# A transformer block in float32 on one core: the two-input instructions of VectorE in another form, GpSimd's order written down, and norms made a tile earlier

## The chip, the core and the metric

The kernel runs on one core of a Trainium2 chip. The metric is the device time of one execution in microseconds (us), lower is better. A core has five engines that run side by side: TensorE (PE, matrix products; its weight loads are listed as PEld), VectorE (DVE), ScalarE (ACT), GpSimd (POOL) and SyncE (SP, which issues most DMAs). Each takes its instructions in one order that is fixed when the program is built, and semaphores make an engine wait for another. SBUF is the memory on chip that all engines work in, PSUM the one that TensorE writes to.

## What is computed

The input `x` has 4 sequences of 2048 tokens with 512 features, in float32. First comes causal attention with one head, then a feed-forward layer with two gates. Cut to what matters here:

```python
h = layernorm(x)
q, k, v = relu(h @ Wq + bq), relu(h @ Wk + bk), relu(h @ Wv + bv)
e = q @ k.T / sqrt(512) - 10000 * causal
y = softmax(e) @ v
x = x + layernorm(relu(y @ Wo + bo))
x = x + layernorm(ffn(layernorm(x)))   # two branches of 512 -> 128 features, softmax, top 32 of 512
```

## The kernel before

**Phases.** `phase1` does the attention, the first residual and the norms for the feed-forward layer; `phase2` does the feed-forward layer and the output. There is a second version of each behind a branch (`every_key=True`) for inputs whose scores could grow too large; it isn't run here.

**Groups.** Phase 1 works on 16 groups of 512 tokens (4 tiles of 128), four groups per sequence; a batch is one sequence here, and `n.g` counts a group in its batch from 0. Features lie on the partitions for q, k, v and scores. The head makes the first group's projections; then `steps` runs a loop over the groups. In one turn, for group `n`: the scores against its own keys (`score_tile`), those against earlier groups' keys, the products of the next group's v, q, k and vo, the maxima, the weights, and the product with the values.

**Products with seven parts.** Except in the head, each 512 x 512 x 512 product is made of seven products of 256-wide halves (`class Seven`, the Strassen-Winograd scheme), which need sums and differences of the halves of both operands. `token_sums`, `value_sums`, `key_sums`, `query_sums` and `last_query_sum` make those on VectorE, one difference each of tokens and queries (T4) on GpSimd. The pieces p1 to p7 are issued on TensorE in the order p2, p5, p1, p3, p6, p7, p4. Several accumulate into one PSUM tile (`acc`), which VectorE writes out in between (`written`, lines 590 and 594): p6, p7 and p4 of a product can't start before the write-out of the piece before.

**Softmax.** `masked` adds the causal mask to the diagonal block (line 680) and takes a running maximum (688); `maximum` does so for the other tiles (577). `fold` and `diagonals` bring the maximum to all partitions, `weights` subtracts it (725, VectorE), takes the exponential (726, ScalarE) and sums (728, 730, GpSimd). `inverses` and `attended` (758) scale the product with the values.

**The chain.** `chain` follows for each tile of a group, while the next group's products run: statistics and inverse root of the variance (`row_norm`: VectorE, then GpSimd at line 140), the norm (771, VectorE), the residual's add into `x1` (773, GpSimd), a second norm (145 to 149, 140, 781), products with the convolution's weights (789, GpSimd), their sums over four features (797, VectorE), transposes (793, 801) and stores. `fetch_features` loads the gates' features back, in another layout, and takes their statistics (276).

**Who sets the order.** TensorE's and VectorE's order in `steps` is the program's (`tc.manual_schedule`); the framework's scheduler orders the other engines. The program's order comes from a planner, `class Pace`. It keeps two clocks: `t`, which every product on TensorE advances, and `v`, VectorE's. VectorE's work is in generators that yield after each piece the piece's time and a pause until the next may come. `run` takes pieces that are due, from three ranks: rank 0 for write-outs and what TensorE waits for, rank 1 for maxima, weights and sums, rank 2 for the chains, of which the first two are open. `flush` issues what is left of a job. The planner knows nothing of what actually happens; it only decides the order.

**Other places.** `moments` takes the statistics of the inputs of the group after next; `transpose_x` makes the norm of the first two groups' tiles on VectorE (319) and transposes them on TensorE (167); later groups go through `turn_x` (328, 331) and DRAM. `prepare` runs in turns 1 and 2: it loads constants of phase 2, one of them (`left`, 859) by a DMA of GpSimd's queue, which VectorE then splits into three rows (862 to 867).

Of the kernel before, what the change touches and what calls it, by code (L numbers as in the profile page):

```python
# [39 lines left out]
P = 128  # L40
GT = 512
# [12 lines left out]
def sandwich_kernel(ctx: ExitStack, tc: tile.TileContext, io: dict, out: bass.AP):  # L54
# [144 lines left out]
    def phase1(every_key):  # L199
# [22 lines left out]
        class Pace:  # L222

            def __init__(self):
                self.t = self.v = 0.0
                self.ranks = [], [], []
# [9 lines left out]
            def step(self, job):  # L239
                try:  # L240
                    us, pause = next(job[1])
                    self.v = max(self.v, job[0]) + us
                    job[0] = self.v + pause
                except StopIteration:
                    for jobs in self.ranks:
                        jobs[:] = [j for j in jobs if j is not job]
# [25 lines left out]
        pace = Pace()  # L272

        def work(us, fn, *args, pause=0.0):

            fn(*args)
            yield us, pause

        def load(b, g):

            n = Group()
            n.b, n.g, n.i = b, g, b * GB + g
            n.x = []
            for t in range(TPG):
                xt = xp.tile([P, D], F32, name="xt")
                row = n.i * GT + t * P
                nc.sync.dma_start(xt, xf[row : row + P, :])
                n.x.append(xt)
            return n

        def moments(n, joint=True):

            n.rstd = sm.tile([P, TPG], F32, name="rstd_x")
            var = sm.tile([P, TPG], F32, name="var_x")
            n.mv = sm.tile([P, TPG, nc.vector.BN_AGGR_DIM], F32, name="mv_x")
            for t, xt in enumerate(n.x):
                st = sm.tile([P, nc.vector.BN_STATS_DIM], F32, name="st_x")
                nc.vector.bn_stats(st, xt)
                nc.vector.bn_aggr(n.mv[:, t, :], st)
                if not joint:  # L300
                    nc.vector.tensor_scalar_add(var[:, t : t + 1], n.mv[:, t, 1:2], LN_EPS)
                    inv_sqrt(n.rstd[:, t : t + 1], var[:, t : t + 1])
                yield 0.8, 0.0
            if joint:
                nc.vector.tensor_scalar_add(var, n.mv[:, :, 1], LN_EPS)  # L305
                inv_sqrt(n.rstd, var)
                yield 0.2, 1.0

        def at_once(pieces):
            for _ in pieces:  # L310
                pass

        def transpose_x(n, tiles=range(TPG)):

            for t in tiles:
                if t == 0:
                    n.xnT = one.tile([P, NC, GT], F32, name="xnT")
                xn = two.tile([P, D], F32, name="xn")
                nc.vector.tensor_scalar(
                    xn, n.x[t], n.mv[:, t, 0:1], n.rstd[:, t : t + 1], ALU.subtract, ALU.mult  # L320
                )
                transposed(ps_tp, xn, n.xnT[:, :, t * P : (t + 1) * P], nc.scalar.copy)

        def turn_x(n):

            for t in range(TPG):
                xn = two.tile([P, D], F32, name="xn")
                nc.vector.tensor_scalar(
                    xn, n.x[t], n.mv[:, t, 0:1], n.rstd[:, t : t + 1], ALU.subtract, ALU.mult
                )  # L330
# [112 lines left out]
        def token_sums(n):  # L443
# [5 lines left out]
            def pieces():  # L449
                nc.vector.tensor_tensor(T1, B12, B11, ALU.subtract)  # L450
                yield 0.75, 0.0
                nc.vector.tensor_tensor(T2, B22, T1, ALU.subtract)
                nc.gpsimd.tensor_tensor(T4, B21, T2, ALU.subtract)
                yield 0.75, 0.0
                nc.vector.tensor_tensor(B12, B22, B12, ALU.subtract)
                yield 0.75, 0.0
# [3 lines left out]
        def value_sums(n, most):  # L460
# [3 lines left out]
            if most:  # L464
                S1, S2 = (one.tile([P, 2, H], F32, name=f"T{k}") for k in (1, 2))
                n.left = {1: A11, 2: A12, 4: A22, 5: S1, 6: S2, 7: A21}
                nc.vector.tensor_tensor(S1, A21, A22, ALU.add)
                yield 0.9, 0.0
                nc.vector.tensor_tensor(S2, S1, A11, ALU.subtract)
                yield 0.9, 0.0  # L470
                nc.vector.tensor_tensor(A21, A11, A21, ALU.subtract)
                yield 0.9, 0.0
            else:
                n.left[3] = one.tile([P, 2, H], F32, name="T4")
                nc.vector.tensor_tensor(n.left[3], A12, n.left[6], ALU.subtract)
                yield 0.9, 0.0

        def key_sums(n):

            A11, A21, A12, A22 = quarters(n.kT)  # L480
            S1, S2, S4 = (one.tile([P, 2, H], F32, name=f"Q{k}") for k in (1, 2, 4))
            nc.vector.tensor_tensor(S1, A21, A22, ALU.add)
            yield 0.9, 0.0
            nc.vector.tensor_tensor(S2, S1, A11, ALU.subtract)
            yield 0.9, 0.0
            nc.vector.tensor_tensor(A21, A11, A21, ALU.subtract)
            yield 0.9, 0.0
            nc.vector.tensor_tensor(S4, A12, S2, ALU.subtract)
            for k, t in ((2, A12), (5, S1), (1, A11), (3, S4), (6, S2), (7, A21), (4, A22)):
# [3 lines left out]
        def query_sums(n):  # L493
# [3 lines left out]
            n.queries = {1: B11, 2: B21, 3: B22, 4: T4, 5: T1, 6: T2}  # L497
            nc.vector.tensor_tensor(T1, B12, B11, ALU.subtract)
            yield 0.9, 0.0
            nc.vector.tensor_tensor(T2, B22, T1, ALU.subtract)  # L500
            nc.gpsimd.tensor_tensor(T4, B21, T2, ALU.subtract)
            yield 0.9, 0.0

        def last_query_sum(n):

            B11, B12, B21, B22 = quarters(n.qT)
            nc.vector.tensor_tensor(B12, B22, B12, ALU.subtract)
            n.queries[7] = B12

        class Seven:  # L510
# [65 lines left out]
            def maximum(self, st):  # L576
                nc.vector.tensor_tensor(self.n.mx, self.n.mx, st, ALU.max)

# [96 lines left out]
        def masked(n, kt):  # L675
            st, off = n.st[kt], first(n, kt)
            own = kt - n.g * TPG
            if 0 <= own < TPG:
                q = slice(own * P, (own + 1) * P)
                nc.vector.tensor_tensor(st[:, q], st[:, q], causal, ALU.add)  # L680
            if every_key and own > 0:
# [5 lines left out]
            else:  # L687
                nc.vector.tensor_tensor(n.mx[:, off:], n.mx[:, off:], st[:, off:], ALU.max)

# [29 lines left out]
        def weights(n):  # L719

            n.sum = one.tile([P, GT], F32, name="mxsum")
            for kt in range(n.nk):
# [6 lines left out]
                else:  # L729
                    nc.gpsimd.tensor_tensor(n.sum[:, off:], n.sum[:, off:], w, ALU.add)  # L730
                yield 0.08 + (GT - off) / 960, 0.0

# [28 lines left out]
        def chain(n, t):  # L761
# [7 lines left out]
            m, r = row_norm(sm, a, "a")  # L769
            yield 1.0, 1.1  # L770
            nc.vector.tensor_scalar(a, a, m, r, ALU.subtract, ALU.mult)
# [4 lines left out]
            store.dma_start(x1_d[n.i][t * P : (t + 1) * P, :], x1)  # L776
            yield 0.55, 1.8
            m, r = row_norm(sm, x1, "x1")
            yield 1.0, 1.1
            xn2 = ap.tile([P, D], F32, name="a")  # L780
# [10 lines left out]
            if not final:  # L791

                nc.vector.transpose(a, xn2)
                nc.sync.dma_start(xn2T_d[n.i][t * P : (t + 1) * P, :], a)
            yield 1.4 if final else 0.7, 0.0 if final else 1.0
            for j, pr in enumerate(prs):
                nc.vector.tensor_reduce(xg[:, j, :], pr.rearrange("p (g f) -> p g f", f=CF), axis=AX.X, op=ALU.add)  # L797
                yield 0.68, 0.0 if final or j else 0.6
            if not final:
# [72 lines left out]
        def steps(n, ahead):  # L872
# [3 lines left out]
            for j in range(NGRP):  # L876
# [88 lines left out]

                pace.flush(weighted)
                if j in (1, 2):
                    next(early)
# [82 lines left out]
        else:  # L1051
# [4 lines left out]
            for m in "vqk":  # L1056
# [4 lines left out]
                drop(w)  # L1061
            w = project_vo(n)
            weight_sums("o", w)
            drop(w)
# [3 lines left out]
            for br in branches:  # L1068
# [303 lines left out]
```

## Time and profile before

| | |
|---|---|
| median of 3 runs | 2513.23 us (2512.48 to 2515.34) |
| profiled execution | 2513.1 us, of which span 2511.3 us from first to last instruction, TensorE's granted clock 0.988 |
| phase 1 / phase 2 | up to about 1813 us / the rest |

Busy time in some stretches of the span (us; a stretch is named by the groups' turns in it):

| stretch | long | PE | DVE | ACT | POOL |
|---|---|---|---|---|---|
| 0 to 90, head and first scores | 90 | 74.5 | 28.1 | 18.3 | 9.0 |
| 90 to 190 | 100 | 93.0 | 70.4 | 30.2 | 29.6 |
| 505 to 640 | 135 | 129.8 | 92.6 | 40.7 | 36.1 |
| 640 to 800 | 160 | 156.8 | 101.6 | 43.6 | 55.7 |
| 800 to 945 | 145 | 145.0 | 84.1 | 36.9 | 46.5 |
| 1760 to 2511, mostly phase 2 | 751 | 710.6 | 690.5 | 540.8 | 607.1 |

A row of the profile's tables of instructions names the line, the engine, the operation, the tile written and the tiles read (buffer numbers left out), the shapes and the count, and then busy time or durations. In the timeline, the first two numbers are start and duration in us, and the bracket at the end is the engine's idle time before the instruction with what ended it. In the waits, a row says who waited for whom, for how long in all, how often, and the longest. Durations come from one execution.

### The profile page before, as it was taken

What the parts mean: (1) busy time and instruction counts of PE and PEld (TensorE: products, weight loads), DVE (VectorE), ACT (ScalarE), POOL (GpSimd) and SP (SyncE); (2) the same over time, 40 slices, a digit from 0 to 9 for tenths busy, and PEclk for the clock granted to TensorE, in tenths of its full rate; (3) what the DMA queues carried; (4) which work ended last, traced back from release to release, by engine and by line L of the source; (5) the groups of instructions that cost most, each with busy time, mean ns of one, the idle gap of its engine ahead of it and who ended that gap; (6) DMA issues with size and microseconds to landing.
All of it is one profiled execution on the core that took longest, in us unless ns stands there. A gap on an engine that the chain in (4) does not pass through costs nothing.

```text
span 2511.3 us, 29224 instructions
## 1 busy us (share of the span) xinstructions
PE 2417.3 (96%) x8354; PEld 1520.5 (61%) x8354; DVE 1777.8 (71%) x3815; ACT 1026.5 (41%) x2232; POOL 1141.6 (45%) x1045
## 2 busy tenths in 40 slices
PE   8989999999999999899999999999899999999997
PEld 3666858587685858668585876856333333333332
DVE  2487675658766565866655577554599999999997
ACT  2323322232332223233131323312178787878785
POOL 1033240423324051342414134231278989898986
PEclk9999999999999999999999999999899999999998
DMA  6577656557765656776555576633424444444541
GB/s 208 165 218 212 196 154 173 147 180 216 208 192 158 169 147 181 225 207 197 162 162 157 175 222 192 190 119 74 122 71 102 110 106 119 107 119 105 120 107 56
DMA packets 594347, 392.18 MB, mean 156 GB/s; under 512 B 392705, under 2 KB 459777, under 8 KB 594177
## 3 DMA queue, kind: packets, MB, share of 16 engines
q1 hardware_dynamic: 590640, 387.05, 55.8%
q10 hardware_dynamic: 3024, 2.11, 0.3%
q8 instruction: 70, 1.15, 0.2%
q0 software_dynamic: 512, 1.06, 0.1%
q14 instruction: 101, 0.82, 0.1%
HBM read 275.26 MB, written 114.82 MB: 155 GB/s over the span
## 4 chain that ended last, share of the span: by engine, by line
PE 80%; DVE 6%; POOL 5%; ACT 4%; issue 4%; DMA 1%; SPq 1%; POOLq 0%; ACTq 0%; DVEq 0%
PE acc L542 20%; PE acc L743 19%; PE mm L542 14%; PE mm L1198 13%; PE mm L660 5%; PE lg L1156 3%; PE mm L397 2%; PE tp L1265 2%; PE lg L1159 1%; POOL e_si L1186 1%; POOL xs L1192 1%; POOL h L1305 1%; ACT L1136 1%; DVE xg L797 1%; POOL x L773 1%
## 5 line engine op out<-in xcount | busy, mean ns | idle before, releaser
L743 PE MATMUL acc<-vo,st 128*128 128x512 f32 x1088 | 474.7, 592 | 1.4 <-ACT st L726 1.4
L743 PEld LDWEIGHTS acc<-vo,st 128*128 128x128 f32 x1088 | 205.3, 190 | 241.5 <-issue 236.0
L1198 PE MATMUL mm<-w_L_ffn_weight,xnT 128*128 128x512 f32 x512 | 249.0, 609 | 0.5 <-ACT xc_si L817 0.5
L1198 PE MATMUL mm<-w_L_ffn_weight,xsT 128*128 128x512 f32 x512 | 239.1, 610 | 2.5 <-ACT xsT L1271 2.5
L140 POOL TENSOR_TENSOR rstd_x<-var_x,neg_half 128x4 f32<-128x4 f32 (+1 forms) x19 | 17.9, 943 | 424.6 <-DVE var_x L305 419.7
L542 PE MATMUL acc<-T,wb 128*128 128x256 f32 x720 | 174.0, 385 | 15.9 <-DVE vT L594 13.4
L140 POOL TENSOR_TENSOR rs_a<-ve_a,neg_half 128x1 f32<-128x1 f32 x64 | 39.2, 613 | 292.6 <-DVE ve_a L149 289.9
L542 PE MATMUL mm<-xnT,wb 128*128 128x256 f32 x720 | 171.1, 381 | 0.0
L730 POOL TENSOR_TENSOR mxsum<-mxsum,st 128x512 f32<-128x512 f32 (+2 forms) x144 | 161.5, 1121 | 13.8 <-ACT st L726 2.9
L542 PE MATMUL acc<-xnT,wb 128*128 128x256 f32 x720 | 165.2, 379 | 0.0
L542 PEld LDWEIGHTS acc<-T,wb 128*128 128x128 f32 x720 | 138.1, 193 | 43.9 <-DVE vT L594 15.0
L1198 PEld LDWEIGHTS mm<-w_L_ffn_weight,xsT 128*128 128x128 f32 x512 | 92.9, 191 | 110.3 <-issue 93.5
L1198 PEld LDWEIGHTS mm<-w_L_ffn_weight,xnT 128*128 128x128 f32 x512 | 92.3, 190 | 106.7 <-issue 106.0
L542 PEld LDWEIGHTS acc<-xnT,wb 128*128 128x128 f32 x720 | 136.8, 190 | 25.0 <-issue 4.3
L542 PEld LDWEIGHTS mm<-xnT,wb 128*128 128x128 f32 x720 | 136.5, 191 | 24.4 <-issue 7.2
L660 PE MATMUL mm<-qT,kT 128*128 128x128 f32 (+3 forms) x512 | 150.2, 437 | 0.0
L561 ACT COPY cp<-mm 128x512 f32<-128x512 f32 x72 | 42.2, 586 | 236.6 <-PE mm L542 236.6
L1164 DVE MAX8 m_si<-rest_si 128x8 f32<-128x512 f32 x192 | 131.3, 684 | 0.0
L1172 DVE MATCH_REPLACE8 rest_si<-m_si,rest_si 128x512 f32<-128x512 f32 x192 | 129.8, 676 | 0.0
L1164 DVE MAX8 m_so<-rest_so 128x8 f32<-128x512 f32 x192 | 129.8, 676 | 0.0
L1172 DVE MATCH_REPLACE8 rest_so<-m_so,rest_so 128x512 f32<-128x512 f32 x192 | 129.8, 676 | 0.0
L590 DVE TENSOR_TENSOR st<-acc,cp 128x256 f32<-128x256 f32 x144 | 54.1, 417 | 102.0 <-PE acc L542 97.9
(245 smaller groups left out, 5056.2 us busy)
## 6 DMA issues: line engine op xcount, KB each, us to landing
wb<-keys SPq DMA_DIRECT2D x168, 256.0 KB, 2.9
x<-x SPq DMA_DIRECT2D x124, 256.0 KB, 3.0
xt<-in_L_attn_x_dram SPq DMA_DIRECT2D x64, 256.0 KB, 3.6
xr<-in_L_attn_x_dram SPq DMA_DIRECT2D x64, 256.0 KB, 3.2
xn<-xn SPq DMA_DIRECT2D x64, 256.0 KB, 2.9
out_dram<-h SPq DMA_DIRECT2D x64, 256.0 KB, 2.0
wb<-Z_v SPq DMA_DIRECT2D x60, 256.0 KB, 3.2
wb<-Z_q SPq DMA_DIRECT2D x60, 256.0 KB, 3.0
```

The costliest lines, as they stand in the source:

```text
L140: nc.gpsimd.tensor_tensor(dst, src, neg_half[:, : src.shape[1]], ALU.pow)
L397: nc.tensor.matmul(ps, lhsT=w[c][1][:, d * P : (d + 1) * P], rhs=xnT[:, c, :], start=(c == 0), stop=(c == NC - 1))
L542: nc.tensor.matmul(ps[:, d * H : (d + 1) * H], lhsT=left[:, c, d * P : (d + 1) * P], rhs=right[:, c, :], start=(new and c + d == 0), stop= ...
L590: nc.vector.tensor_tensor(st[:, cols], acc[:, d, :], other[:, d, :], ALU.add)
L660: nc.tensor.matmul(ps[:, off:], lhsT=kT[:, c, k : k + P], rhs=n.qT[:, c, off:], start=(c == 0), stop=(c == NC - 1),)
L730: nc.gpsimd.tensor_tensor(n.sum[:, off:], n.sum[:, off:], w, ALU.add)
L743: nc.tensor.matmul(acc, lhsT=n.st[kt][:, t * P : (t + 1) * P], rhs=vos[kt // TPG][:, kt % TPG, :], start=(kt == 0), stop=(kt == nk - 1),)
L1156: nc.tensor.matmul(n.lg[br], lhsT=xa[n.k][br][:, n.t * P : (n.t + 1) * P], rhs=lin_T[br], start=True, stop=False)
L1164: nc.vector.max(n.m8[br], n.rest[br] if k else n.lg[br])
L1172: nc.vector.match_replace(n.rest[br], n.m8[br], n.rest[br], -LOWEST)
L1198: nc.tensor.matmul(ps, lhsT=lhsT[:, c, :], rhs=wf[:, c, :], start=(c == 0), stop=(c == NC - 1))
L1265: nc.tensor.transpose(tp[:, c, :], p.xs[:, c * P : (c + 1) * P], ident)
```

## The change

- A helper `combine(out, a, b, op)` issues `scalar_tensor_tensor` on VectorE, (a times 1.0) op b. In the groups' steps it takes the place of `tensor_tensor` wherever both inputs lie in SBUF: `token_sums`, `value_sums`, `key_sums`, `query_sums`, `last_query_sum`, `maximum` and `masked`. Instructions with an input in PSUM (590, 594, 725) stay, as do the head's `weight_sums` and phase 2.
- GpSimd joins the engines whose order in `steps` is the program's. The planner gets a third clock, `p`, GpSimd's; a piece may yield a tuple in place of its pause: the times of what it issues on GpSimd, of which the first is what the next piece waits for.
- The norms of the second group's tiles: two are made in the head, before `weight_sums("o", ...)`, and kept in `n.ahead`; in the loop each of the others is issued a tile before its transposes. The transposes of token tile `t` follow the scores of key tile `t`; before, those of tiles 0 and 1 followed key tile 0, those of 2 and 3 key tiles 1 and 2.
- The flush of the chains that are left of the group before (`behind`) and `fetch_features` move from before K's products to behind the flush of the weights.

```diff
             def step(self, job):
                 try:
-                    us, pause = next(job[1])
+                    us, behind = next(job[1])
                     self.v = max(self.v, job[0]) + us
-                    job[0] = self.v + pause
+                    job[0] = self.v + behind if isinstance(behind, float) else max(self.p, self.v + 0.2) + behind[0] + 0.1
+                    if not isinstance(behind, float):
+                        self.p = max(self.p, self.v + 0.2) + sum(behind)
...
+        def combine(out, a, b, op):
+
+            nc.vector.scalar_tensor_tensor(out, a, 1.0, b, ALU.mult, op)
...
             if joint:
                 nc.vector.tensor_scalar_add(var, n.mv[:, :, 1], LN_EPS)
                 inv_sqrt(n.rstd, var)
-                yield 0.2, 1.0
+                yield 0.2, (0.55,)
...
+        def normed(n, t):
+            xn = two.tile([P, D], F32, name="xn")
+            nc.vector.tensor_scalar(xn, n.x[t], n.mv[:, t, 0:1], n.rstd[:, t : t + 1], ALU.subtract, ALU.mult)
+            return xn
...
-                xn = two.tile([P, D], F32, name="xn")
-                nc.vector.tensor_scalar(
-                    xn, n.x[t], n.mv[:, t, 0:1], n.rstd[:, t : t + 1], ALU.subtract, ALU.mult
-                )
+                xn = n.ahead.pop(0) if n.ahead else normed(n, t)
                 transposed(ps_tp, xn, n.xnT[:, :, t * P : (t + 1) * P], nc.scalar.copy)
...
-                nc.vector.tensor_tensor(T2, B22, T1, ALU.subtract)
+                combine(T2, B22, T1, ALU.subtract)
                 nc.gpsimd.tensor_tensor(T4, B21, T2, ALU.subtract)
+                pace.p = max(pace.p, pace.v + 1.0) + 1.4
...
             def maximum(self, st):
-                nc.vector.tensor_tensor(self.n.mx, self.n.mx, st, ALU.max)
+                combine(self.n.mx, self.n.mx, st, ALU.max)
...
                     nc.gpsimd.tensor_tensor(n.sum[:, off:], n.sum[:, off:], w, ALU.add)
+
+                pace.p = max(pace.p, pace.v + 1.3) + 0.1 + (GT - off) / 450
                 yield 0.08 + (GT - off) / 960, 0.0
...
             m, r = row_norm(sm, a, "a")
-            yield 1.0, 1.1
+            yield 1.0, (0.55,)
...
-            yield 0.55, 1.8
+            yield 0.55, (1.27,)
             m, r = row_norm(sm, x1, "x1")
-            yield 1.0, 1.1
+            yield 1.0, (0.55,)
...
-            yield 1.4 if final else 0.7, 0.0 if final else 1.0
+            yield (1.4, 0.0) if final else (0.7, (1.27, 1.27))
             for j, pr in enumerate(prs):
                 nc.vector.tensor_reduce(xg[:, j, :], pr.rearrange("p (g f) -> p g f", f=CF), axis=AX.X, op=ALU.add)
-                yield 0.68, 0.0 if final or j else 0.6
+                yield 0.68, 0.0 if final or j else 1.0
...
                 for t in range(TPG):
+                    if nxt is not None and nxt.i == 1 and t:
+                        transpose_x(nxt, ([0], [1], [2])[t - 1])
+                        if t < 3:
+                            nxt.ahead.append(normed(nxt, t + 1))
                     score_tile(n, n.g * TPG + t, n.kT)
...
-                    if nxt is not None and nxt.i == 1:
-                        transpose_x(nxt, ([0, 1], [2], [3], [])[t])
-                        if t == TPG - 1:
-                            tokens = pace.add(0, token_sums(nxt))
+                if nxt is not None and nxt.i == 1:
+                    transpose_x(nxt, [3])
+                    tokens = pace.add(0, token_sums(nxt))
...
                 weighted = pace.add(1, weights(n))
-                if before is not None:
-                    pace.flush(*behind)
-                    fetch_features(before.i)
...
                 pace.flush(weighted)
+                if before is not None:
+                    pace.flush(*behind)
+                    fetch_features(before.i)
...
             w = project_vo(n)
+            ahead.ahead = [normed(ahead, t) for t in range(2)]
             weight_sums("o", w)
...
-            with tc.manual_schedule(engines={PE, mybir.EngineType.DVE}):
+            with tc.manual_schedule(engines={PE, mybir.EngineType.DVE, mybir.EngineType.Pool}):
                 steps(n, ahead)
```

More of the change, by code (lines that the diff above doesn't have):

```diff
@@ L227, in __init__ @@
             def __init__(self):
-                self.t = self.v = 0.0
+                self.t = self.v = self.p = 0.0
                 self.ranks = [], [], []
@@ L282, in load @@
             n.b, n.g, n.i = b, g, b * GB + g
-            n.x = []
+            n.x, n.ahead = [], []
             for t in range(TPG):
@@ L326, in turn_x @@
             for t in range(TPG):
[L327 to L330, printed above, removed]
+                xn = normed(n, t)
                 nc.vector.transpose(n.x[t], xn)
@@ L449, in pieces @@
             def pieces():
-                nc.vector.tensor_tensor(T1, B12, B11, ALU.subtract)
+                combine(T1, B12, B11, ALU.subtract)
                 yield 0.75, 0.0
-                nc.vector.tensor_tensor(T2, B22, T1, ALU.subtract)
+                combine(T2, B22, T1, ALU.subtract)
                 nc.gpsimd.tensor_tensor(T4, B21, T2, ALU.subtract)
+                pace.p = max(pace.p, pace.v + 1.0) + 1.4
                 yield 0.75, 0.0
-                nc.vector.tensor_tensor(B12, B22, B12, ALU.subtract)
+                combine(B12, B22, B12, ALU.subtract)
                 yield 0.75, 0.0
@@ L466, in value_sums @@
                 n.left = {1: A11, 2: A12, 4: A22, 5: S1, 6: S2, 7: A21}
-                nc.vector.tensor_tensor(S1, A21, A22, ALU.add)
+                combine(S1, A21, A22, ALU.add)
                 yield 0.9, 0.0
-                nc.vector.tensor_tensor(S2, S1, A11, ALU.subtract)
+                combine(S2, S1, A11, ALU.subtract)
                 yield 0.9, 0.0
-                nc.vector.tensor_tensor(A21, A11, A21, ALU.subtract)
+                combine(A21, A11, A21, ALU.subtract)
                 yield 0.9, 0.0
@@ L474, in value_sums @@
                 n.left[3] = one.tile([P, 2, H], F32, name="T4")
-                nc.vector.tensor_tensor(n.left[3], A12, n.left[6], ALU.subtract)
+                combine(n.left[3], A12, n.left[6], ALU.subtract)
                 yield 0.9, 0.0
@@ L481, in key_sums @@
             S1, S2, S4 = (one.tile([P, 2, H], F32, name=f"Q{k}") for k in (1, 2, 4))
-            nc.vector.tensor_tensor(S1, A21, A22, ALU.add)
+            combine(S1, A21, A22, ALU.add)
             yield 0.9, 0.0
-            nc.vector.tensor_tensor(S2, S1, A11, ALU.subtract)
+            combine(S2, S1, A11, ALU.subtract)
             yield 0.9, 0.0
-            nc.vector.tensor_tensor(A21, A11, A21, ALU.subtract)
+            combine(A21, A11, A21, ALU.subtract)
             yield 0.9, 0.0
-            nc.vector.tensor_tensor(S4, A12, S2, ALU.subtract)
+            combine(S4, A12, S2, ALU.subtract)
             for k, t in ((2, A12), (5, S1), (1, A11), (3, S4), (6, S2), (7, A21), (4, A22)):
@@ L497, in query_sums @@
             n.queries = {1: B11, 2: B21, 3: B22, 4: T4, 5: T1, 6: T2}
-            nc.vector.tensor_tensor(T1, B12, B11, ALU.subtract)
+            combine(T1, B12, B11, ALU.subtract)
             yield 0.9, 0.0
-            nc.vector.tensor_tensor(T2, B22, T1, ALU.subtract)
+            combine(T2, B22, T1, ALU.subtract)
             nc.gpsimd.tensor_tensor(T4, B21, T2, ALU.subtract)
+            pace.p = max(pace.p, pace.v + 1.0) + 1.4
             yield 0.9, 0.0
@@ L506, in last_query_sum @@
             B11, B12, B21, B22 = quarters(n.qT)
-            nc.vector.tensor_tensor(B12, B22, B12, ALU.subtract)
+            combine(B12, B22, B12, ALU.subtract)
             n.queries[7] = B12
@@ L679, in masked @@
                 q = slice(own * P, (own + 1) * P)
-                nc.vector.tensor_tensor(st[:, q], st[:, q], causal, ALU.add)
+                combine(st[:, q], st[:, q], causal, ALU.add)
             if every_key and own > 0:
@@ L687, in masked @@
             else:
-                nc.vector.tensor_tensor(n.mx[:, off:], n.mx[:, off:], st[:, off:], ALU.max)
+                combine(n.mx[:, off:], n.mx[:, off:], st[:, off:], ALU.max)
         def no_scores(n):
```

## The prediction

> **What bounds the kernel now.** I read the page first, then the windows by stage, then the waits of TensorE, and last the timeline in front of each of those waits.
>
> ```profile
> PE 2417.3 (96%) x8354; PEld 1520.5 (61%) x8354; DVE 1777.8 (71%) x3815; ACT 1026.5 (41%) x2232; POOL 1141.6 (45%) x1045
> PE 80%; DVE 6%; POOL 5%; ACT 4%; issue 4%; DMA 1%; SPq 1%; POOLq 0%; ACTq 0%; DVEq 0%
> ```
>
> TensorE carries 80% of the chain that ended last. The change touches phase 1 alone, which runs to about 1813 us; the rest is VectorE's top-k and stays. In phase 1 only time in which TensorE stands still can be won, and the waits of TensorE say how much that is:
>
> ```profile
> PE acc L542 <- DVE vo L594: 17.3, 10, 2.1
> PE tp L167 <- DVE xn L319: 14.8, 4, 8.9
> PE acc L542 <- DVE vT L594: 13.4, 4, 3.8
> PE acc L542 <- DVE st L590: 3.1, 3, 1.1
> PE acc L542 <- DVE qT L594: 2.4, 3, 1.2
> PE acc L743 <- ACT st L726: 1.4, 1, 1.4
> ```
>
> The columns are total, times, longest. 8.9 of the second row is the start, before any group. The steps' stalls are 17.3 + 5.9 + 13.4 + 3.1 + 2.4 + 1.4 = 43.5 us, 1.7% of the span: no more than that is to be had. Almost all end with VectorE (DVE) writing a product out late (L594), though those writes take 0.69 us as ever. So I looked at what VectorE did before them, first ahead of the `vo` stall in a batch's second group:
>
> ```profile
> 588.39 1.26 POOL L789 TENSOR_TENSOR pr<-a,convw_so 128x512 f32<-128x512 f32 x1
> 588.53 1.27 DVE L680 TENSOR_TENSOR st<-st,causal 128x128 f32<-128x128 f32 x1
> 589.62 1.32 POOL L789 TENSOR_TENSOR pr<-a,convw_si 128x512 f32<-128x512 f32 x1
> 589.84 1.38 DVE L688 TENSOR_TENSOR mxsum<-mxsum,st 128x256 f32<-128x256 f32 x1
> ...
> 596.78 0.91 PE L542 MATMUL acc<-wb,vT 128*128 128x256 f32 x3 [1.96 <-DVE vo L594]
> ```
>
> L680 has a median of 0.29 us; here it ends only when GpSimd (POOL) ends, and so does L688 (0.43 at that size alone). Between 584 and 597 these rows lose 3.45 us to it, more than the stall of 1.96. Second, ahead of the `vT` stall and of the `vo` stall in the third group:
>
> ```profile
> 614.58 0.70 DVE L145 BATCH_NORM_STATS2 st_x<-x 128x6 f32<-128x512 f32 x1 [2.46 <-POOL x L773]
> 617.40 3.05 DVE L577 TENSOR_TENSOR mxsum<-mxsum,st 128x512 f32<-128x512 f32 x2
> 620.37 0.68 DVE L594 TENSOR_TENSOR vT<-acc,x 128x512 f32<-128x512 f32 x1
> ```
> ```profile
> 693.16 0.70 DVE L145 BATCH_NORM_STATS2 st_x<-x 128x6 f32<-128x512 f32 x1 [3.08 <-POOL x L773]
> 694.77 0.68 DVE L594 TENSOR_TENSOR vo<-acc,st 128x512 f32<-128x512 f32 x1
> ```
>
> VectorE runs in program order. The planner put the second norm of a chain 1.8 us after L771, but GpSimd still had 2.5 us of `pr` before its add, so VectorE stood and the write-out stood behind it.
>
> **The change, part by part.** By cause the 43.5 us are:
> - A, transposes of group 1 behind L319: 2.01 + 2.04 + 1.80 = 5.9.
> - B, `vo` of the second groups behind blocked two-input instructions: 4 x 1.96 = 7.8; no GpSimd wait ahead.
> - C, `vT`: 3.8 + 3 x 3.2 = 13.4, behind 1.56 of blocking and 2.46 to 3.07 of waiting for GpSimd.
> - D, `vo` of the third groups: 2.05 + 3 x 2.0 = 8.1, behind 3.09 of waiting for GpSimd and no blocking.
> - E, two `vo` of 0.68 and two `st` of 1.11: 3.6, behind both.
> - F, `qT`: 2.4, behind statistics of features (L276) that wait 1.44 for their DMA.
> - G, the last group: 0.85 + 1.44 = 2.3.
>
> *The form.* 397 instructions of VectorE get it (L577 96, L680 64, L688 48, the sums of tokens, values, keys and queries 189). 56 of them are blocked in this profile and lose 38 us of VectorE together. No scalar-tensor-tensor with both inputs in SBUF and more than one element is in the trace, so its cost is bounded:
>
> ```profile
> L577 DVE TENSOR_TENSOR mxsum<-mxsum,st x96: 679/692/1564, 170.6 to 1737.7; 128x512 f32<-128x512 f32 x96
> L758 DVE SCALAR_TENSOR_TENSOR st<-acc,rsum,r_L_attn_bo x48: 731/750/753, 127.1 to 1674.9; 128x512 f32<-128x512 f32 x48
> L188 DVE SCALAR_TENSOR_TENSOR q<-tot,q x1: 147/147/147, 2493.4 to 2493.4; 1x1 f32<-1x1 f32 x1
> ```
>
> L758 (one input in PSUM, a scalar per partition) takes 0.06 more than 0.69; L188, with a constant and both in SBUF, takes the same 147 ns as the tensor-tensor before it (L187). Alone I take 0.69, nearest to L188; the ends are 0.69 and 1.56, the longest that any such row shows. L758 keeps to 0.75 beside a running GpSimd too, but it has one SBUF input, so it doesn't settle whether the form waits. I take it that it doesn't: then B goes whole, 7.8, and the 1.56 in C and the blocked part of E go too. If it does wait, none of that goes; below nothing isn't excluded for single instructions, since GpSimd, no longer held up, starts its next one earlier.
>
> [...]
>
> *GpSimd's clock in the planner.* Chain steps are now due when GpSimd's queue, as modelled, has done their input. Write-outs come before chains in rank, so they no longer stand behind those waits: the GpSimd part of C (13.4 less 6.2), D, the `st` part of E. Which piece fills the hole I can't tell without its order; F too hangs on order, as `fetch_features` and the flush of the chains move behind the weights. I count C to F, 27.5, at two thirds: 18.3. The ends are 0 and 27.5.
>
> *Norms a tile ahead.* A: two norms are made before the loop, the others a tile early, so the score copies that hold them up now (L680 waits 0.4, 3.9 and 4.6 for ScalarE) are out of the way. The fourth tile's transposes now stand right ahead of p2 of `v`; from there T1 needs a copy of 0.59 and 0.68 of VectorE, under p2's 1.73. I take 5.3.
>
> *GpSimd in written order: what it is moved past.* `prepare`'s load of `left` (L859) was issued at 175.0 and 267.6; the rows that need it ran at 208.1 and 317.0. Written down, it stands behind the groups' sums of weights, which ended at 209.7 and 322.9. With 0.6 to issue and at least 1.2 more to land, VectorE's cast L862 starts some 4 and 8 us late, and queued behind it are `kT`'s write-out and the inverses. TensorE reaches the product that needs that `kT` at 217.6 and 329.5; the write-out ended at 215.8 and 324.5. It comes 2 and 3.5 late: 6 us with the landing's spread, once in the run. Chain pieces that are left over when weights begin now follow GpSimd's backlog (last L725 at 204.3, sums to 209.7: 5.4 us). Only the second groups have any today (one L797 and one L801, no GpSimd in front). I take 0.5 in each of four, 2 us; the ends are 0 and 4 x 5.
>
> Sum: 5.3 + 7.8 + 18.3 - 6 - 2 = 23.4 off the profiled execution's 2513.1 (span 2511.3 and 1.8 around it; the median is 2513.2): 2490.
>
> **The rivals.**
> 1. The form waits as before. What is left is A, 5.3, and two thirds of C's GpSimd part, D, `st` and F (7.2 + 8.1 + 2.2 + 2.4 = 19.9), 13.3; with the costs of 8 that is 10.6 off: 2502. For it: two inputs must be read somehow. Against: nothing in the trace.
> 2. The form itself is slow, and the run is slower than before. Place: VectorE without slack, 14 of these instructions between 584 and 621 and 6 between 688 and 702, 80 over four batches. If each takes x more, TensorE gets 80x later; from x = 0.29 (0.98 us for 512 elements) it eats the 23.4. At the upper end, 0.87 more, it is 70 - 23: 2560. Against it L188's 147 ns, which is one element and can't show a rate.
> 3. The written order gives back what it brings: A and B and C's blocked part (19.3), nothing from the plan, the 6, and 5 in each second group (20): 7 over, 2520. For it: GpSimd's backlog behind 8 to 16 sums of 1.28 against VectorE's 0.68.
>
> **How the numbers follow.** Forecast 0.50, rivals 0.21, 0.14 and 0.15. The range: below, all of A to F but no cost is 40.6, 2472; above, it takes in rival 1 and most of rival 3: 2471 to 2527, with rival 2 left out. The forecast's own range is 2472 to 2505. A measurement here can tell about 0.2%, 5 us, from no change. Faster: 0.95 of the forecast and 0.8 of rival 1, 0.65. Slower: rival 2 and most of rival 3, 0.27. Same: 0.08.
>
> **What would show it.** Right: L577, L680 and L688 with no row much over 0.7 while GpSimd runs; no `vo` wait near 597; L145's wait for `x` gone from ahead of L594; the transposes of group 1 without idle. Wrong: converted rows near 1 us or more alone (rival 2), or up to 1.5 beside GpSimd (rival 1); L862 or L797 waiting for GpSimd or its DMA by more than 8 us, with TensorE behind (rival 3). A change in phase 2's 700 us would break the frame of it all.

## The result and the profile after

The changed kernel takes 2490.25 us (2489.02 to 2491.48, 4 runs) beside 2512.86 us of the kernel before (2512.01 to 2515.34): the ratio is 0.9908, 95% interval 0.9891 to 0.9926. That is 22.6 us less. The forecast was 2490. The number was met; the mechanism that it put first, the form, did not work.

The profiled execution after has a span of 2487.3 us (2511.3 before) and a granted clock of 0.992 (0.988). Its page, busy time by engine and the chain that ended last:

```profile
PE 2405.2 (97%) x8354; PEld 1513.4 (61%) x8354; DVE 1787.4 (72%) x3815; ACT 1026.1 (41%) x2232; POOL 1143.6 (46%) x1045
...
PE 70%; POOL 4%; ACT 4%; DVE 4%; issue 3%; DMA 2%; SPq 1%; POOLq 0%; ACTq 0%; DVEq 0%
```

The instructions are as many as before, engine by engine. VectorE's busy time has not fallen (1777.8 before) and GpSimd's neither: nothing got faster by itself. The waits of TensorE after (total, times, longest, in us):

```profile
PE tp L167 <- DVE xn L322: 8.9, 1, 8.9
PE acc L550 <- DVE vo L602: 8.2, 12, 1.9
PE acc L550 <- POOL rs_x L140: 6.9, 3, 2.6
PE acc L550 <- POOL pr L799: 4.7, 1, 4.7
PE acc L550 <- DVE kT L602: 4.5, 2, 4.1
...
PE acc L753 <- ACT st L734: 1.4, 1, 1.4
```

The row for `xn` is down to the start's 8.9, so group 1's transposes no longer wait. The 13.4 for `vT` and the 17.3 for `vo` have shrunk to 8.2, but new names stand beside them: `rs_x` and `pr` of GpSimd, and one `kT` of 4.1.

Measured to the end of the last product with the values, phase 1 went from 1796.5 to 1769.5 us, 27.0 less; the rest of the span went from 714.8 to 717.8. Counted one by one, TensorE's stalls above 0.45 us in phase 1 (from 60 us on, behind the start) fell from 43.5 us (24 stalls) to 24.4 (12), 19.1 less. The other part is a term that the prediction did not have. The granted clock falls to 0.50 for 3.41 us at or just after some long stalls, and each such stretch loses 1.7 us: 8 before (13.7 us), 3 after (5.1), 8.6 less. Two smaller terms nearly cancel: TensorE's idle times of 0.45 us and less grew from 0.2 to 3.1 us in all, 2.9 more, and the first scores of the profiled execution start at 68.4 in place of 70.6 us, 2.1 less. The latter is not the change's doing: the granted clock's record begins at 12.5 in place of 17.6 us, the head's first products start 0.86 us apart until then in the kernel before and 0.43 in the kernel after, and no_form below, the same change without the form, starts them at 70.6. 19.1 + 8.6 + 2.1 − 2.9 make 26.9 for the 27.0.

### The profile page after: what moved, and what is told of

The parts are those of the page before. It is cut to its first block, busy times and chain, and to the rows that moved or that the text cites. A ratio compares the mean times of both kernels' runs of the same rounds, so it can differ in the third digit from the quotient of the medians.

```text
span 2487.3 us, 29206 instructions
## 1 busy us (share of the span) xinstructions
PE 2405.2 (97%) x8354; PEld 1513.4 (61%) x8354; DVE 1787.4 (72%) x3815; ACT 1026.1 (41%) x2232; POOL 1143.6 (46%) x1045
## 4 chain that ended last, share of the span: by engine, by line
PE 70%; POOL 4%; ACT 4%; DVE 4%; issue 3%; DMA 2%; SPq 1%; POOLq 0%; ACTq 0%; DVEq 0%
PE acc L550 18%; PE acc L753 17%; PE mm L550 12%; PE mm L1212 12%; PE mm L668 3%; PE lg L1170 3%; PE tp L1279 1%; PE lg L1173 1%; POOL e_si L1200 1%; POOL xs L1206 1%; POOL h L1319 1%; DMA xr<-in_L_attn_x_dram 1%; ACT L1150 1%; DVE xg L807 1%; POOL x L783 1%
## 5 line engine op out<-in xcount | busy, mean ns | idle before, releaser
L279 DVE SCALAR_TENSOR_TENSOR mxsum<-mxsum,st 128x512 f32<-128x512 f32 (+2 forms) x144 | 100.7, 699 | 67.2 <-ACT st L596 62.5
```

Of the source, the lines that this page charges most:

```text
L279: nc.vector.scalar_tensor_tensor(out, a, 1.0, b, ALU.mult, op)
```

## The experiments

Times are medians; each ratio is against the kernel before on the same chip, with its 95% interval. "Stalls" are those of phase 1 as above, "stretches" those at half clock; both come from the profiled execution. The first theory (T) was that the form does nothing and that the order does all: the norms ahead and the planner's clock for GpSimd. Its rivals were the prediction's own reading (F), that the form ends the blocking, and that GpSimd's written order carries the gain (W).

| kernel | us | ratio | stalls, us | stretches |
|---|---|---|---|---|
| the change | 2490.25 | 0.9908 [0.9891, 0.9926] | 24.4 | 3 |
| form_only | 2513.58 | 0.9996 [0.9987, 1.0005] | 43.2 | 4 |
| no_form | 2490.88 | 0.9911 [0.9898, 0.9925] | 23.0 | 3 |
| pool_by_scheduler | 2492.46 | 0.9909 [0.9892, 0.9926] | 25.3 | 3 |
| old_pauses | 2491.31 | 0.9911 [0.9897, 0.9924] | 26.8 | 7 |
| flush_back | 2493.70 | 0.9919 [0.9906, 0.9933] | 29.1 | 5 |
| norms_only | 2502.78 | 0.9962 [0.9948, 0.9975] | 36.0 | 7 |
| norms_flush | 2497.72 | 0.9934 [0.9920, 0.9947] | 36.4 | 7 |
| norms_written | 2509.54 | 0.9979 [0.9968, 0.9989] | 36.1 | 9 |
| norms_xr | 2490.98 | 0.9910 [0.9894, 0.9925] | 26.1 | 3 |
| left_on_act | 2487.71 | 0.9902 [0.9889, 0.9916] | 22.4 | 2 |
| xr_on_act | 2478.92 | 0.9861 [0.9846, 0.9876] | 17.0 | 1 |
| all_on_act | 2471.69 | 0.9830 [0.9816, 0.9843] | 12.6 | 0 |

### The form alone, and the change without it

form_only is the kernel before with the form in all 397 places and nothing else:

```diff
+        def combine(out, a, b, op):
+            nc.vector.scalar_tensor_tensor(out, a, 1.0, b, ALU.mult, op)
...
-                nc.vector.tensor_tensor(T1, B12, B11, ALU.subtract)
+                combine(T1, B12, B11, ALU.subtract)
```

> The kernel before with the scalar-tensor-tensor form alone. Theory T (the form changes nothing; the planner's third clock brings the gain): no change, 2513 within 2 us, and L577's successor still has rows of 1.4 to 1.57 us beside GpSimd. Theory F (the prediction's: the form doesn't wait for GpSimd): the 38 us of blocking on VectorE are gone, and with them B 7.8, 6.2 of C and 1.4 of E: about 2498.

no_form is the change with the old instruction inside the helper:

```diff
-            nc.vector.scalar_tensor_tensor(out, a, 1.0, b, ALU.mult, op)
+            nc.vector.tensor_tensor(out, a, b, op)
```

> The changed kernel with tensor-tensor put back, everything else kept. T: no change against the changed kernel, 2490 within 2 us. F: 10 to 15 us slower than the changed kernel, 2500 to 2505, with the vo stalls of the second groups back.

The form alone gives 0.9996 and cannot be told from no change; without it the change is as good as with it. Both are T's numbers, and F fell. The timeline of form_only at the place that the prediction showed for tensor-tensor (start, duration, engine, line; the bracket is TensorE's idle time):

```profile
587.69 1.27 POOL L792 TENSOR_TENSOR pr<-a,convw_so 128x512 f32<-128x512 f32 x1
587.82 1.28 DVE L275 SCALAR_TENSOR_TENSOR st<-st,causal 128x128 f32<-128x128 f32 x1
588.91 1.31 POOL L792 TENSOR_TENSOR pr<-a,convw_si 128x512 f32<-128x512 f32 x1
589.14 1.38 DVE L275 SCALAR_TENSOR_TENSOR mxsum<-mxsum,st 128x256 f32<-128x256 f32 x1
...
596.07 1.99 PE L545 MATMUL acc<-wb,vT 128*128 128x256 f32 x8 [1.96 <-DVE vo L597]
```

The mask's add of 0.29 us ends with GpSimd's instruction once more, and the stall of 1.96 is the same to the hundredth. In the changed kernel the row of the running maximum gives shortest, median and longest in ns:

```profile
L279 DVE SCALAR_TENSOR_TENSOR mxsum<-mxsum,st x144: 291/692/1510, 75.9 to 1710.6; 128x512 f32<-128x512 f32 x96, 128x384 f32<-128x384 f32 x16, 128x256 f32<-128x256 f32 x16, 128x128 f32<-128x128 f32 x16
```

So the form takes 0.69 us when nothing is beside it, as tensor-tensor did, and up to 1.51 in this row. Of the 397 instructions, those that run over 0.12 us past their own time are blocked ones: 56 that lose 38 us before, 56 with 38 in form_only, and 60 with 39 both in the change and in no_form.

### The other parts, taken out one at a time

```diff
-            with tc.manual_schedule(engines={PE, mybir.EngineType.DVE, mybir.EngineType.Pool}):
+            with tc.manual_schedule(engines={PE, mybir.EngineType.DVE}):
```

> The changed kernel with GpSimd's order left to the framework's scheduler; VectorE's and TensorE's order stay as changed. T: the written order itself brings nothing; it costs the stall behind prepare in turn 1 (4.1 us of TensorE and perhaps 1.7 of clock), so this one is about 6 faster, 2484. Theory W (the written order is what keeps GpSimd from doing things too late): it falls back by 5 us or more, to 2495 or above.

```diff
-            yield 1.0, (0.55,)
+            yield 1.0, 1.1
...
-            yield 0.55, (1.27,)
+            yield 0.55, 1.8
...
-                yield 0.68, 0.0 if final or j else 1.0
+                yield 0.68, 0.0 if final or j else 0.6
```

> The changed kernel with the chain's and the moments' old fixed pauses in the planner (GpSimd's order still written down, the form, the norms ahead and the moved flush kept). T: the waits of VectorE for GpSimd's x come back, and with them the vT and vo stalls (C 13.4 and D 8.1) and several stretches of half clock: 2490 plus 15 to 25, 2505 to 2515. F and W: it stays at 2490 to 2495, since form and written order are still there.

```diff
                 weighted = pace.add(1, weights(n))
+                if before is not None:
+                    pace.flush(*behind)
+                    fetch_features(before.i)
...
                 pace.flush(weighted)
-                if before is not None:
-                    pace.flush(*behind)
-                    fetch_features(before.i)
```

> The changed kernel with the flush of the chains and fetch_features back ahead of K's products. T: the qT waits behind statistics that wait for their DMA come back (F, 2.4 us), and the left-over chain pieces stand ahead of the weights: 2 to 6 us slower than the changed kernel, 2492 to 2496. Rival: the flush hardly matters, 2490 within 1.5.

Neither the written order nor the planner's clock is missed by itself: 0.9909 and 0.9911 cannot be told from the change's 0.9908. T had given the planner's clock most of the gain, and that fell; so did W, and T's 2484 without the written order. Without the moved flush some 3 us go, inside the intervals. That is T's range, but not T's reason: no `qT` wait over 0.45 us came back. What grew are the four stalls that the change has under the names of `pr` (4.7) and `rs_x` (6.9), 11.6 us in all, to 19.4. The timeline of flush_back ahead of one of them:

```profile
604.91 1.26 POOL L783 TENSOR_TENSOR x<-st,xr 128x512 f32<-128x512 f32 x1 [6.96 <-DMA xr<-in_L_attn_x_dram]
...
606.21 0.69 DVE L145 BATCH_NORM_STATS2 st_x<-x 128x6 f32<-128x512 f32 x1 [5.47 <-POOL x L783]
...
607.22 0.74 DVE L598 TENSOR_TENSOR st<-acc,cp 128x256 f32<-128x256 f32 x2
...
608.07 1.19 PE L550 MATMUL acc<-Q,wb 128*128 128x256 f32 x2 [5.94 <-POOL pr L799]
```

TensorE's 5.94 is put down to `pr`, but read upward: the write-out (L598) stood behind a norm that waited 5.47 for GpSimd's add, and GpSimd had stood idle for 6.96 for `xr`, the residual's rows on their way from DRAM. That is not a busy GpSimd. It raised a new theory: the late thing is a load.

### The residual's load on another queue

`xr` is issued on SyncE's queue in the piece that takes the statistics before the norm. The timeline of the changed kernel around the second of its four stalls of this kind:

```profile
596.79 0.97 SPq L778 DMA_DIRECT2D xr<-in_L_attn_x_dram  x2
...
601.30 2.65 POOL L783 TENSOR_TENSOR x<-st,xr 128x512 f32<-128x512 f32 x2 [3.01 <-DMA xr<-in_L_attn_x_dram]
...
602.60 0.69 DVE L145 BATCH_NORM_STATS2 st_x<-x 128x6 f32<-128x512 f32 x1 [1.74 <-POOL x L783]
...
604.99 0.75 DVE L598 TENSOR_TENSOR st<-acc,cp 128x256 f32<-128x256 f32 x2
...
605.84 3.21 PE L550 MATMUL acc<-Q,wb 128*128 128x256 f32 x8 [2.53 <-POOL rs_x L140]
```

The two loads are issued at 596.8 and 597.3, among the other loads of SyncE's queue, and land at 601.1 and 602.5; the norms had ended at 597.9 and 598.9. The add can't start, VectorE waits for it, and the write-out that TensorE needs is queued behind. In the kernel before, 8 of the 64 loads land after the norm that they go with, by 30 us in all. The timeline of before, one of those:

```profile
607.93 0.42 SPq L768 DMA_DIRECT2D xr<-in_L_attn_x_dram  x1
...
612.04 1.27 POOL L789 TENSOR_TENSOR pr<-a,convw_si 128x512 f32<-128x512 f32 x1
613.27 1.27 POOL L773 TENSOR_TENSOR x<-st,xr 128x512 f32<-128x512 f32 x1
```

This is the add that the prediction said stood behind `pr`. It did; but its rows landed at 612.5, so without any `pr` it would have come 0.8 us earlier at most. xr_on_act is the change with one word more; norms_only is the kernel before with the norms ahead alone (the change's `normed`, `n.ahead` and the new places of the transposes), and norms_xr adds the same word to that:

```diff
-            nc.sync.dma_start(xr, xf[ti * P : (ti + 1) * P, :])
+            nc.scalar.dma_start(xr, xf[ti * P : (ti + 1) * P, :])
```

> The changed kernel with the residual's load xr on ScalarE's DMA queue. If the stalls at 166, 606, 1037 and 1468 us (4.7 + 2.5 + 1.8 + 2.6 = 11.6) come from GpSimd's add waiting for xr, whose load stands behind ring loads in SyncE's queue: 8 to 14 us faster, 2476 to 2482. If they come from the two buffers of xr, which the products also use, or from the DMA engines' load: no change within 2, or slower by ScalarE's issue time.

> The kernel before with the norms a tile ahead alone. Prediction's step A: the three idle times of 2.0 us at group 1's transposes go, 5.3 us; as the half-clock stretch at 82.4 us stands right behind them, 1.7 more: 2506 to 2508. Rival: the transposes only move a wait to T1 and p5, and the time stays at 2513.

> The kernel before with the norms ahead and the load of xr on ScalarE's DMA queue, nothing of the plan. Theory X (the waits of VectorE for GpSimd's x are at bottom xr's late landing: in the profile before, 8 of 64 loads land after the norm that the add goes with, by 4.2 and 3.1 us ahead of the vT and vo stalls): the vT stalls (13.4) lose their 2.5 to 3.1 of waiting, the third groups' vo (8) go: 2502.8 less 15 to 20, 2483 to 2488, better than the whole change. The prediction's reading (the add stands behind GpSimd's products, the load is hidden): no change, 2501 to 2505.

On ScalarE's queue the loads are issued some 20 us earlier (tile 18: 573.8 in place of 596.8) and none of the 64 lands late, in either kernel. VectorE's waits for the add, before, after and in xr_on_act:

```profile
DVE st_x L145 <- POOL x L773: 43.9, 31, 3.1
```
```profile
DVE st_x L145 <- POOL x L783: 24.7, 25, 4.2
```
```profile
DVE st_x L145 <- POOL x L783: 13.6, 19, 1.4
```

The time follows: 2478.92 in place of the change's 2490.25, as expected, and the four stalls are down to one of 1.3 and three of 1.0. That SyncE's queue is also shorter by these 64 loads was not tried apart from their earlier issue. The norms ahead alone give 0.9962, 9.9 us, more than the 7 that were expected of them. From there the one word brings 0.9910, as much as form, planner's clock, written order and moved flush do together. Theory X's 2483 to 2488 was still missed by 3 us. The waits of TensorE in norms_xr say why:

```profile
PE acc L544 <- DVE vo L596: 13.1, 8, 2.7
...
PE acc L544 <- DVE qT L596: 7.3, 4, 2.5
...
PE acc L544 <- DVE vT L596: 3.8, 4, 1.6
```

`vT` fell from 13.4 in norms_only to 3.8, and the third groups' `vo` stalls of 2.0 are gone. But `qT` grew from 1.3 to 7.3, in four, and `vo` still takes 13.1: its stalls in the second groups grew from 2.0 to 2.7 each. Why those grew was not followed.

### Moved flush and written order, each with the norms only

norms_flush adds to norms_only the new place of the flush and of `fetch_features`; norms_written adds Pool to the engines in program order.

> The kernel before with the norms ahead and the moved flush (with fetch_features); old pauses, GpSimd by the scheduler, tensor-tensor. Theory M (moving the flush reorders VectorE's steps and SyncE's loads so that the chain's second pair starts earlier; the other two parts of the plan only do the same in another way): most of the 12 us that norms_only left, 2490 to 2494. Theory S (the parts add up, a third each): about 2499.

> The kernel before with the norms ahead and GpSimd's order written down; VectorE's and TensorE's order as in norms_only. M: nothing but the late load of left: 2503 to 2508, with GpSimd's add ahead of the products now waiting for xr itself. S, or a written order that matters by itself: 2499 or less.

By the times the flush brings about half of what is missing (0.9934), near S and not M. The profiled execution does not show where: stalls and stretches come to the same as in norms_only, and 2.1 of the 4.1 us by which its phase 1 is shorter lie ahead of the first scores. It takes three of the four stalls for `vT` and three of the four `vo` stalls of the second groups away, and puts others in their place (`vo` 20.5 in nine). The written order alone seems to lose against norms_only: 0.9979 and 0.9962, with intervals that just overlap, and it is 1.5 us above M's range. Its stalls are the same in sum, with 16.2 for `vT` in place of 13.4, and it has two more stretches at half clock (17.1 us lost, 13.7 in norms_only). The timelines of GpSimd show what the order does. First norms_only, then norms_written, at the same chain pieces:

```profile
682.37 1.27 POOL L791 TENSOR_TENSOR pr<-a,convw_so 128x512 f32<-128x512 f32 x1 [1.63 <-DVE a L783]
683.60 1.27 POOL L791 TENSOR_TENSOR pr<-a,convw_si 128x512 f32<-128x512 f32 x1
684.83 1.27 POOL L775 TENSOR_TENSOR x<-st,xr 128x512 f32<-128x512 f32 x1
```
```profile
687.43 1.26 POOL L775 TENSOR_TENSOR x<-st,xr 128x512 f32<-128x512 f32 x1 [2.58 <-DMA xr<-in_L_attn_x_dram]
688.65 1.27 POOL L791 TENSOR_TENSOR pr<-a,convw_so 128x512 f32<-128x512 f32 x1
```

The framework's scheduler puts two `pr` first, while `xr` is on its way; in program order the add stands first and GpSimd idles 2.58 for the load, with `pr` behind, later than it was. With the flush moved, it is the other way round. First norms_flush, then old_pauses, which differs in the written order (and in the form):

```profile
602.78 0.55 POOL L140 TENSOR_TENSOR rs_a<-ve_a,neg_half 128x1 f32<-128x1 f32 x1 [3.32 <-DVE ve_a L149]
603.30 1.26 POOL L775 TENSOR_TENSOR x<-st,xr 128x512 f32<-128x512 f32 x1
```
```profile
600.58 1.27 POOL L783 TENSOR_TENSOR x<-st,xr 128x512 f32<-128x512 f32 x1 [1.25 <-DVE st L781]
602.64 0.55 POOL L140 TENSOR_TENSOR rs_a<-ve_a,neg_half 128x1 f32<-128x1 f32 x1 [0.79 <-DVE ve_a L149]
```

Here both inputs of the add were there at 600.6. The scheduler had put the next tile's `rs_a` ahead of it, so GpSimd idled 3.32; written down, the add goes first, 2.7 us sooner. That is one tile read in two traces, not a run of its own. The planner's clock alone with the norms was not tried, so how flush, written order and planner's clock share the 12 us between norms_only and the change stays open.

### What `prepare` lost, and a best version

```diff
-            nc.gpsimd.dma_start(left, io[f"L0_ffn_{br}_lin_b"].rearrange("(o n) -> o n", o=1))
+            nc.scalar.dma_start(left, io[f"L0_ffn_{br}_lin_b"].rearrange("(o n) -> o n", o=1))
```

> The changed kernel with prepare's load of left on ScalarE's DMA queue in place of GpSimd's. Prediction's cost of the written order (load behind the weights' sums, kT's write-out late, 4.1 us of TensorE idle at 209.9, then a half-clock stretch): 4 to 6 us faster, 2484 to 2486. Rival: the wait for the rows' own DMA (6.1 us on SyncE's queue) keeps the stall, and it stays at 2490.

The stall stayed, 4.2 us at 212, and the time (0.9902) cannot be told from the change's. The timeline of the change shows what VectorE waited for:

```profile
195.99 0.58 POOL L869 DMA_DIRECT2D st<-in_L_ffn_so_lin_b_dram  x1
...
199.00 0.41 DVE L872 CAST row<-st 1x512 bf16<-1x512 f32 x1 [2.80 <-DMA st<-in_L_ffn_so_lin_b_dram]
...
202.56 2.08 SPq L158 DMA_DIRECT2D xc_si<-xgT  x4
204.74 0.60 SPq L873 DMA_DIRECT2D lin_so<-row  x1
...
206.69 0.42 DVE L872 CAST row<-st 1x512 bf16<-1x512 f32 x1 [6.11 <-DMA lin_so<-row]
...
209.18 0.67 DVE L602 TENSOR_TENSOR kT<-acc,x 128x512 f32<-128x512 f32 x1
```

`left` costs VectorE 2.80, but the second cast waits 6.11 until the first row has been carried away on SyncE's queue. That row was ready at 199.4; its store was issued at 204.74, behind the loads of `fetch_features` (L158), which the moved flush puts there. So this stall does not need the written order: pool_by_scheduler, where `left` had landed at 172.5, and norms_flush, which has neither written order nor planner's clock, have it too, and norms_written, where VectorE waits 4.14 for `left`, does not. TensorE's waits for `kT` in these three:

```profile
PE acc L550 <- DVE kT L602: 4.1, 1, 4.1
```
```profile
PE acc L544 <- DVE kT L596: 4.7, 1, 4.7
```
```profile
PE acc L544 <- DVE kT L596: 0.6, 2, 0.3
```

With the flush back, `left` does it: in flush_back the first cast waits 6.97 for it, and TensorE's longest wait for `kT` is 3.3. In the change either cause suffices. all_on_act puts the rows on ScalarE's queue as well, with `xr` and `left`:

```diff
-                nc.sync.dma_start(lin_3[br][k : k + 1, :], row)
+                nc.scalar.dma_start(lin_3[br][k : k + 1, :], row)
```

> The changed kernel with xr, left and the rows' stores all on ScalarE's DMA queue. X, with the rest of prepare's stall (3.9 us of TensorE at 208 and a half-clock stretch) gone too: 2472 to 2475. If that stall has another cause: 2479 as with xr alone.

2471.69 us, 0.9830: the best version, ahead of both kernels and at the lower edge of what was expected. Its waits of TensorE in the steps:

```profile
PE acc L550 <- DVE st L598: 8.7, 8, 1.3
PE acc L550 <- DVE vo L602: 5.6, 14, 1.0
...
PE acc L753 <- ACT st L734: 1.4, 1, 1.4
```

No stall is over 1.4 us any more, `kT` and `pr` are gone, and there is no stretch at half clock in phase 1. Against the change, stalls fell by 11.8 and the clock's loss by 5.1, and phase 1 became 16.7 us shorter (1752.8).

## Why the prediction was right, and where it wasn't

- **The forecast, 2490.** Right in the total (2490.25), and that is luck: its terms erred in both directions, and 8.6 us came from a term that it did not have. The step that failed is the one where "I take it that it doesn't [wait]". It waits: rival 1's condition held, and B's 7.8 and two thirds of the 7.6 that C and E owed to blocking, 12.9 us in all, were credited to the form and did not come from it. Rival 1's own 2502 missed too, because it had B stay (the new order took it away, 6.8) and did not have the clock (8.6).
- **The form's cost.** Beside GpSimd's product the mask's add took 1.28 us in this form too, in place of 0.29. With nothing beside it the form took 0.69 us for 512 elements, no slower than tensor-tensor, so rival 2 had no footing.
- **A, 5.3.** Right: 5.8 of `xn` stalls went to 0. norms_only gained 9.9 us, with 7.5 less in stalls; where the rest of the 9.9 comes from is open.
- **B, 7.8.** It went to 1.0, but by order: in norms_flush the moved flush took three of the four away. VectorE is blocked as much as ever in the change (39 us in all), but less of it lies ahead of that write-out: at the place that the prediction showed, between 584 us and the write-out, 1.1 us in the change and 0.2 in norms_flush, where it had counted 3.45.
- **C and D, 21.5, two thirds of the GpSimd part.** They came to 16.9, a gain of 4.6; with E and F, C to F gave 10.6 for the 18.3. The prediction read the wait for `x` as GpSimd's `pr`, one step short of its root: the landing of `xr` on SyncE's queue. A planner that counts GpSimd's queue cannot see that load; 12 of 64 land late after (one of them by 0.15 us), 8 before. xr_on_act shows it.
- **E and F, 3.6 and 2.4.** Both to 0. G stayed at 2.3, as it was left out of the sum.
- **`prepare`, 6.** Right in size by luck: one stall of 4.1 in turn 1 with a stretch of 1.7 behind it, none in turn 2, where 3.5 had been expected. The late `left` that the prediction saw is real, but the moved flush brings the same stall without it, through the row's store on SyncE's queue.
- **Leftover chains, 2.** Nothing came of it.
- **The missing term.** 5 fewer stretches at half clock, 8.6 us. Part of it is chance: form_only has 4 fewer with the same stalls.
- **The rest, behind phase 1**, became 3.0 us longer. 1.8 of it lies behind TensorE's last instruction (12.8 us in place of 10.9); no row explains why, and among the experiments the rest lies between 713.6 and 718.7 us, with 715.3 in the best version.

So 5.8 + 6.8 + 4.6 + 3.6 + 2.4 − 4.1 = 19.1 of stalls, 8.6 of clock and 2.1 at the start, less 2.9 in short idle times and 3.0 in the rest, make 23.9 of the 24.0 by which the spans differ. The prediction's 23.4 held 12.9 for a form that did nothing, too little for what the moved work does, and nothing for the clock.

## What to carry to other kernels

A wait that ends with a busy-looking engine is followed one step further: ask what that engine's instruction itself waited for, and above all when its DMA was issued and when it landed. A load that belongs to a chain wants a queue on which it can be issued long before it is needed; here a word per load brought 11.8 us (norms_only to norms_xr), as much as a change to planner, order and form. A change with several parts is worth runs of its parts: here one that was credited with 12.9 us did nothing, and three others can each be left out at a loss of some 3 us or less.

## What was not expected of the hardware

A stall of TensorE sometimes cost more than its length here, 1.7 us more in the stretch behind it. The windows of before and of form_only over the same stretch, after a stall of 1.96 us in both (window, length, busy time and count of PE, PEld, DVE, ACT and POOL, granted clock, DMA share, GB/s):

```profile
597.90:601.30 3.40, 3.40 (x10) 2.69 (x9) 3.29 (x8) 0.00 (x0) 0.64 (x2) 0.50 0.44 149
```
```profile
597.90:601.30 3.40, 3.40 (x17) 2.85 (x15) 3.29 (x8) 0.00 (x0) 1.34 (x2) 1.00 0.23 88
```

At 0.50 the window lists 10 matmuls, those at its edges included, at 1.00 it lists 17; inside it a product starts 0.43 us after the one before, and 0.22 at 1.00. In phase 1 of the fourteen profiles each stretch lasted 3.41 or 6.83 us, had a stall of 1.9 us or more beside it, and not every such stall had one: with the same stalls there were 8 stretches before and 4 in form_only, and their spans differ by 3.6 us.

The traces tell when. In each of the fourteen profiles all changes of the granted clock lie whole multiples of 3.413 us apart; in the kernel before, 82.44 and 184.84 are 30 of them apart. Cut phase 1 at these points, from some 55 us on, and add up TensorE's idle time in each piece, short gaps too. Of the 6974 pieces at full clock, 61 have 1.94 us of it or more, and every one of them is followed by a piece at half clock; of the six between 1.88 and 1.94 one is, and of the others none. So in these profiles a stall of some 2 us cost the extra 1.7 only where it fell into one piece nearly whole. In the example above, TensorE stands idle from 594.82 to 596.78 in the kernel before, inside the piece that ends at 597.86; in form_only it does from 594.11 to 596.07, and a border at 594.59 leaves 0.48 on one side and 1.48 on the other.
